# Transposing token tiles on VectorE in 32 by 32 blocks instead of on TensorE, in a cross-attention and expert-routing kernel

## The chip, the cores and the metric

The kernel runs on one core of a Trainium2 chip. The metric is the device time of one execution in microseconds. Engines are called by their names or as the profile shortens them: PE is TensorE (PEld its weight loads), DVE is VectorE, ACT is ScalarE, POOL is GpSimd, SP is SyncE, which issues most DMAs.

## The reference

Two blocks follow each other over x, four batches of 1024 tokens with 1024 features, all in float32. First an attention whose map comes from a context alone:

```python
query = einsum('bnc,dc->bnd', ctx, Wq) + bq          # 128 features
key = einsum('bnc,dc->bnd', ctx, Wk) + bk
attention = softmax(einsum('bnd,bmd->bnm', query, key))
x = x + einsum('bln,bmn->blm', layernorm(x), attention)
```

So a token's normed features are the contracted side, and each output feature m has a row of the attention. Then a mixture of experts on the normed x:

```python
xt = layernorm(x).reshape(4096, 1024)
scores = sigmoid(xt @ gate_w.T)                        # 8 experts
_, sel = top_k(scores + expert_bias, 2)
shared = (silu(xt @ sw1.T) * (xt @ sw3.T)) @ sw2.T     # hidden 704
routed = each chosen expert's swiglu of (score * xt), in bf16
x = x + shared + the routed rows added at their tokens
```

## The kernel before, in words

The tokens are 32 tiles of 128, worked in pairs g, g+1. The kernel has three stages: the attention (to about 621 us), the shared experts (eight blocks s of 512 tokens) and the routed experts (23 slots).

**Orders.** In the attention, the order of TensorE, GpSimd, VectorE and ScalarE is the order of the program text (manual_schedule, lines 218 and 553): each runs its instructions in order, and one that waits holds all that stand behind it. SP's DMAs there are ordered by the framework; in the shared experts SP's are in text order too.

**A pair.** product (line 399) multiplies a pair's two tiles, seen as a 2 by 2 block matrix, by the attention map, with seven block products instead of eight. seven (line 197) issues the seven steps k = 0 to 6, eight matmuls each, into three PSUM banks pa, pb, pc of which pa serves four times. After each step VectorE adds the bank's contents, times the token's inverse deviation rs, into the tile (line 410), and then between(k) puts other work in the text. A bank has one buffer, so the next use of it waits for that add. The step's stationary sides are the transposed tokens and sums of them: row_sums (line 391) makes three sums and a difference on GpSimd, of which step 1 needs the first. The products with the batch map need five such combinations of it: first_sums and second_sum on VectorE (lines 353, 360), last_sums on GpSimd.

**What rides along.** While batch b is multiplied, the map of batch b+1 is made: two 128-row strips a pair. For a strip, energies (line 317) puts four matmuls on TensorE and a row maximum nm on VectorE, softmax (line 326) is an exp with a sum on ScalarE, scaled (line 333) a reciprocal rc on VectorE and a product on ScalarE, turned (line 342) eight TensorE transposes in two PSUM tiles pt and two ScalarE copies out. Strip i is begun at the head of the pair, strip i+1 at k = 2; they are turned at k = 3 and 4. At a batch's first pair, queries makes the queries and keys first. In the last batch none of this is there.

**A tile's own path.** load brings x in. tokens (line 379) turns it on TensorE by transposed (line 250): for each half of the features four transposes into a PSUM tile pt (two buffers) and a ScalarE copy out. statistics (line 262) takes mean and variance on VectorE, and pow and a product on GpSimd give rs and nb; first_norm adds nb on ScalarE. After the product, stored (line 421) writes the tile to x2d in DRAM and takes its statistics; second_norm (line 426) makes the normed tile xt on ScalarE; turn (line 434) transposes xt on TensorE by the same helper into xtT, which is stored to xtd for the shared experts. gate_parts and gate (lines 444, 456) make the gate's logits from xtT with an eviction gs on ScalarE between them, route (line 460) the two chosen experts on VectorE, counts and lists_of their places in the lists. weighted (line 521) makes the two rows of each token, xt times its score, one on ScalarE and one on VectorE; scatter writes them to the lists with indirect DMAs.

**Conversions.** convert(e) (line 242) issues three DMAs on GpSimd's queue that read one expert's weights from DRAM in float32 and write them in bf16. Six experts are converted in the attention (pairs p = 1, 3, 5, 7, 10, 13, at k = 1), the other two in the shared experts at blocks s = 0 and 1 (line 1115).

**Lists read back.** From block 1 on, turns (line 978) gathers list rows with GpSimd's indirect DMAs (xgt), two ahead; VectorE reads the token number out of each (toks, line 999), and SP issues a transposing DMA. Two gathers are issued at the end of block 1's first half; the next ones in text order stand behind block 1's convert. Steps of turns stand between those of up (line 914).

Of the kernel before, what the change touches and what calls it, by code (L numbers as in the profile page):

```python
# [39 lines left out]
P = 128  # L41
# [21 lines left out]


# [13 lines left out]
def xattn_moe_kernel(ctx: ExitStack, tc: tile.TileContext, x, ctxT, wqT, wkT, bqk, gwT, ebias,  # L78
# [8 lines left out]
    x2d = dram.tile([T, D], F32, name="x2d")  # L87
# [137 lines left out]
    HALF, KH, M = KC // 2, NF // 2, NF * P  # L225
    LT = S // P
    with ExitStack() as a:
# [34 lines left out]
        def statistics(src, n):  # L262
# [9 lines left out]
            rs = sm.tile([P, 1], F32, tag="rs", name=f"rs_{n}", bufs=8)  # L272
            nc.gpsimd.tensor_tensor(rs, ve[:, 1:], const("half"), ALU.pow)  # L273
            nb = sm.tile([P, 1], F32, tag="nb", name=f"nb_{n}", bufs=8)
            nc.gpsimd.tensor_tensor(nb, ve[:, :1], rs, ALU.mult)
            return rs, nb
# [20 lines left out]
        def half_queries(b):  # L297
            for h in range(2):
# [13 lines left out]
                for i, to in enumerate((qs, ks)):  # L312
                    nc.vector.tensor_scalar_add(
                        to[b][:, cols], pq[:, i].rearrange("p j n -> p (j n)"), bqk_sb[:, i : i + 1])
# [57 lines left out]
        xin, xTs, x1s, xts, norms = {}, {}, {}, {}, {}  # L372

        def load(g):
            x1 = p3.tile([P, D], F32, tag="x1", name=f"x1_{g}", bufs=4)
            nc.sync.dma_start(x1, x[g * P : (g + 1) * P, :])
            xin[g] = x1

        def tokens(g):
            xTs[g] = [p3.tile([P, HALF, P], F32, tag=f"x{g % 2}{h}", name=f"xT_{g}_{h}")  # L380
                      for h in range(2)]
            transposed(xTs[g], xin[g], f"x{g}")

        def first_norm(g):

            x1 = xin.pop(g)
            rs, nb = norms.pop(g)
            nc.scalar.activation(x1, x1, AF.Identity, bias=nb)
            x1s[g] = x1, rs
# [31 lines left out]
        def stored(g):  # L421
            x1 = x1s[g][0]
            nc.sync.dma_start(x2d[g * P : (g + 1) * P, :], x1)
            norms[g] = statistics(x1, f"2_{g}")

        def second_norm(g):
            x2 = x1s.pop(g)[0]
            rs, nb = norms.pop(g)
            xts[g] = xt = p2.tile([P, D], F32, tag="xt", name=f"xt_{g}", bufs=4)
            nc.scalar.activation(xt, x2, AF.Identity, bias=nb, scale=rs)  # L430

        xtTs = {}

        def turn(g):

            if g % 2 == 0:
                xtTs[g] = p2.tile([P, KC, 2 * P], F32, tag="xtT", name=f"xtT_{g}", bufs=1)
            cols = slice(g % 2 * P, (g % 2 + 1) * P)
            xtT = xtTs[g - g % 2]
            transposed([xtT[:, :HALF, cols], xtT[:, HALF:, cols]], xts[g], f"t{g}")  # L440
            if g % 2:
# [79 lines left out]
        def weighted(g, i, ss):  # L521
            xt = xts.pop(g + i)
            rr = p2.tile([P, 2, ROW], BF16, tag="rr", name=f"rr_{g}_{i}")
            nc.scalar.mul(rr[:, 0, :D], xt, ss[:, 0, i : i + 1])
            nc.vector.tensor_scalar_mul(rr[:, 1, :D], xt, ss[:, 1, i : i + 1])
# [5 lines left out]
        def scatter(g, tois, rrs):  # L531
            for i in range(G):
                for k in range(2):
# [3 lines left out]
                        in_=rrs[i][:, k, :].bitcast(I32), in_offset=None)  # L537

# [13 lines left out]
        load(0)  # L552
        with tc.manual_schedule(engines=vector_scalar):
            ps_e = psum("ps_e", 3)
            for dst, k in ((trib, "tri"), (onesb, "ones")):
                nc.vector.tensor_copy(dst, const(k))
            halves = queries(0)
            tokens(0)
# [4 lines left out]
            nc.sync.dma_start(gw_sb[:, :, :E], gwT)  # L563

            sel = wp.tile([P, E], F32, name="sel")
            nc.vector.tensor_reduce(sel, ident.rearrange("p (j r) -> p r j", j=4)[:, :E, :], AX.X,
                                    ALU.add)
            eb_sb = wp.tile([P, E], F32, name="eb_sb")
            nc.sync.dma_start(eb_sb, ebias)
            next(halves)  # L570
            load(1)
            norms[1] = statistics(xin[1], "1_1")
# [11 lines left out]
            next(halves)  # L584
            first_sums(0)
# [4 lines left out]
            routing, listing, pair = {}, {}, {}  # L590
            for p in range(NT // 2):
# [19 lines left out]
                tokens(g + 1)  # L611
                first_norm(g + 1)
                a_units = row_sums(g)
# [6 lines left out]
                if p:  # L620
                    if ahead:
                        turn(g - 2)
                    second_norm(g - 1)
                if not new:
                    softened(i)

                def between(k):
                    if k == 0:
                        if not ahead:
                            turn(g - 2)  # L630
                        if new:
                            next(halves)
                        if p > 1:
                            pc_, ss, ohs = listing[g - 4]
                            listing[g - 4] = lists_of(g - 4, pc_, ohs), ss
                        if g + 2 < NT:
                            load(g + 2)
                            load(g + 3)
                        if g == NT - LT:
                            nc.sync.dma_start(sw13_sb, sw13)  # L640
                    elif k == 1:
# [3 lines left out]
                        if p:  # L645
                            turn(g - 1)
                        if ahead:
                            scaled(b + 1, i, on_scalar=True)
                        if p > 1:
                            tois, ss = listing.pop(g - 4)  # L650
                            listing[g - 4] = tois, [weighted(g - 4, j, ss) for j in range(G)]
                        if p in (1, 3, 5, 7, 10, 13):
                            convert((1, 3, 5, 7, 10, 13).index(p))
                    elif k == 2:
                        if not ahead:
                            pair[g] = gate_parts(g - 2)
                        looked(i + 1)
                        softened(i + 1)
                        if g + 2 < NT:
# [5 lines left out]
                    elif k == 3:  # L665
                        if p:
                            gs = gate_parts(g - 2) if ahead else pair.pop(g)
# [611 lines left out]
```

## Time and profile before

| | us |
|---|---|
| median of three runs | 1972.87 |
| lowest and highest | 1968.97, 1973.47 |
| the profiled execution, its time | 1973.84 |
| its span, first to last instruction | 1972.0 |
| TensorE busy in the span | 1940.1 |
| VectorE busy | 810.4 |
| ScalarE busy | 512.9 |
| GpSimd busy | 653.0 |

A group line of the profile gives source line, engine, operation, output tile and input tiles with their shapes, the count, then busy time in us, mean ns of one, and the idle time of the engine just before them with what ended it. A line of the order of time gives start and duration in us, engine, line and operation. A line of waits gives who waited for whom, us in total, how often, and the longest. A line of the table of stretches gives each engine's busy time and number of instructions in the stretch, TensorE's granted clock, the DMA engines' busy share and GB/s. Where a helper issues the work (line 129 for matmuls, line 256 for transposes, line 260 for their copies), tile names tell what it is: pt_x are transposes of x, pt_t of xt, pt_a of the attention.

### The profile page before, as it was taken

How to read it: one execution, taken by the hardware profiler on the slowest of the kernel's cores; microseconds unless marked ns; L12 is line 12 of the kernel's file. 1: busy time of each engine (PE TensorE's matmuls, PEld its weight loads, DVE VectorE, ACT ScalarE, POOL GpSimd, SP SyncE). 2: the span in 40 equal slices, each digit the busy share in tenths (PEclk: the TensorE clock that was granted, in tenths of full speed). 3: DMA queues.
4: the chain of work that ended last, by engine and by line, in shares of the span. 5: the costliest groups of instructions: out<-in, count | busy, mean ns of one | idle time of the engine just before them, and what ended most of it. 6: DMA issues, size and time to landing. Idle time of an engine off the chain costs nothing.

```text
span 1972.0 us, 23197 instructions
## 1 busy us (share of the span) xinstructions
PE 1940.1 (98%) x8480; PEld 1155.5 (59%) x8595; DVE 810.4 (41%) x1981; ACT 512.9 (26%) x884; POOL 653.0 (33%) x598
## 2 busy tenths in 40 slices
PE   8999999999999999999999999999999999999997
PEld 5655655655444447676676758584845555446564
DVE  5556566565875325423132323222233333223343
ACT  3344354355334101010111101010102233223242
POOL 0423533543642140313231222313014454425454
PEclk9999999999999999999999999999999999999999
DMA  3276485437685225397777868596464598649995
GB/s 124 65 194 169 167 220 158 154 129 206 246 228 203 98 75 141 94 238 205 202 187 191 206 179 224 153 173 193 121 265 107 114 311 275 140 131 326 342 357 98
DMA packets 225040, 365.48 MB, mean 185 GB/s; under 512 B 114080, under 2 KB 169888, under 8 KB 214048
## 3 DMA queue, kind: packets, MB, share of 16 engines
q0 software_dynamic: 43024, 172.78, 32.8%
q1 hardware_dynamic: 181904, 191.21, 32.0%
q8 instruction: 69, 1.13, 0.2%
q14 instruction: 43, 0.35, 0.1%
HBM read 289.19 MB, written 174.59 MB: 235 GB/s over the span
## 4 chain that ended last, share of the span: by engine, by line
PE 89%; DMA 5%; SPq 2%; DVE 2%; issue 1%; ACT 0%; POOL 0%; POOLq 0%; DVEq 0%; ACTq 0%
PE pa L129 19%; PE bank L129 15%; PE pc L129 10%; PE bank L1151 8%; PE qa L129 6%; PE pb L129 5%; DMA xh<-xgt 4%; PE pu L129 4%; PE pq L308 3%; PE pe L320 3%; PE qc L129 3%; PE pt_c L129 2%; PE pt_a L256 2%; SPq L1004 2%; PE qb L129 1%; PE pt_t L256 1%
## 5 line engine op out<-in xcount | busy, mean ns | idle before, releaser
L129 PE MATMUL bank<-xTb,w 128*128 128x0 bf16 x2024 | 311.6, 315 | 2.1 <-ACT sg_b L145 1.3
L129 PEld LDWEIGHTS <-w 128*128 128x128 bf16 x2024 | 190.5, 98 | 111.5 <-DVE hTb L1135 1.3
L749 POOL DMA_INDIRECT xgt<-xrows,li x92 | 88.8, 965 | 444.2 <-DMA xh<-xgt 211.6
L1184 POOL DMA_INDIRECT out_dram<-yt,toks x92 | 147.7, 1605 | 139.5 <-DVE yt L1180 80.8
L1151 PE MATMUL bank<-w,hTb 128*128 128x0 bf16 x920 | 164.5, 326 | 0.1
L273 POOL TENSOR_TENSOR rs<-ve,con 128x1 f32<-128x1 f32 x64 | 47.8, 747 | 313.7 <-DVE ve L271 313.7
L146 DVE TENSOR_TENSOR hTb<-sg_b,bank 128x512 bf16<-128x512 f32 x115 | 78.8, 688 | 161.5 <-PE bank L129 157.2
L129 PE MATMUL pa<-xs,sw_sb 128*128 128x256 f32 x560 | 132.3, 379 | 0.0
L1151 PEld LDWEIGHTS <-hTb 128*128 128x128 bf16 x920 | 72.4, 98 | 87.4 <-issue 11.7
L129 PE MATMUL pa<-aT,xT 128*128 128x512 f32 x256 | 116.8, 599 | 2.2 <-DVE x L410 2.0
L129 PEld LDWEIGHTS pa<-xs,sw_sb 128*128 128x128 f32 x560 | 106.4, 190 | 14.5
L145 ACT ACTIVATE sg_b<-bank 128x512 f32<-128x512 f32 x115 | 68.5, 597 | 165.8 <-PE bank L129 150.2
L1180 DVE COPY yt<-bank 128x512 f32<-128x512 f32 x92 | 61.3, 689 | 121.9 <-PE bank L1151 112.5
L1182 ACT COPY yt<-bank 128x512 f32<-128x512 f32 x92 | 53.3, 587 | 144.1 <-PE bank L1151 131.7
L749 POOL DMA_INDIRECT w<-w13b,wi x23 | 23.0, 999 | 201.4 <-PE bank L129 153.6
L534 POOL DMA_INDIRECT xrows<-rr,toi x64 | 64.9, 1015 | 60.9 <-issue 45.3
L410 DVE SCALAR_TENSOR_TENSOR x<-pa,rs,x 128x512 f32<-128x512 f32 x64 | 47.9, 748 | 88.8 <-PE pa L129 82.9
L166 ACT ACTIVATE st_c<-pt_c 64x256 f32<-64x256 f32 x7 | 2.6, 378 | 311.0 <-PE pt_c L129 311.0
L266 DVE BATCH_NORM_STATS2 st<-x 128x6 f32<-128x512 f32 x128 | 81.8, 681 | 0.6
L1032 DVE TENSOR_TENSOR x2c<-x2c,qa 128x512 f32<-128x512 f32 x64 | 43.8, 685 | 92.4 <-PE qa L129 92.4
L129 PE MATMUL pu<-xb,sw_sb 128*128 128x512 f32 x176 | 76.3, 593 | 0.9 <-PE pt_t L256 0.9
L941 DVE TENSOR_TENSOR one<-one,pb 128x256 f32<-128x256 f32 x35 | 14.7, 421 | 149.4 <-PE pb L129 140.1
(262 smaller groups left out, 3346.5 us busy)
## 6 DMA issues: line engine op xcount, KB each, us to landing
xturned<-xh SPq DMA_DIRECT2D x46, 512.0 KB
xTb<-xturned SPq DMA_DIRECT2D x23, 1024.0 KB
w13b<-in_w_dram POOLq DMA_DIRECT2D x8, 2816.0 KB
x<-in_x_dram SPq DMA_DIRECT2D x32, 512.0 KB
x2d<-x SPq DMA_DIRECT2D x32, 512.0 KB
xtd<-xtT SPq DMA_DIRECT2D x16, 1024.0 KB
xb<-xtd SPq DMA_DIRECT2D x8, 2048.0 KB
x2c<-x2d SPq DMA_DIRECT2D x16, 1024.0 KB
```

The costliest lines, as they stand in the source:

```text
L129: nc.tensor.matmul(part(pp), w(c), part(xT(c)), start=start and c == 0, stop=c == blocks - 1, skip_group_check=not start)
L145: nc.scalar.activation(sg, pa, AF.Silu)
L146: nc.vector.tensor_tensor(hT[:, f, :], sg, pb, ALU.mult)
L256: nc.tensor.transpose(pt[:, j, :], src[:, c * P : (c + 1) * P], ident)
L266: nc.vector.bn_stats(st[:, h, :], src[:, h * 512 : (h + 1) * 512])
L308: nc.tensor.matmul(pq[:, i, j, :], w[c // CH][:, c % CH, :], ct[c // CH][:, c % CH, :], start=c == 0, stop=c == CC - 1)
L320: nc.tensor.matmul(pe[:, h, :], qs[b][:, m * P : (m + 1) * P], ks[b][:, h * 512 : (h + 1) * 512], start=True, stop=True)
L534: nc.gpsimd.indirect_dma_start(out=places[2 * (g + i) + k], out_offset=bass.IndirectOffsetOnAxis(ap=tois[k][:, i : i + 1], axis=0), in_=rr ...
L749: nc.gpsimd.indirect_dma_start(out=dst, out_offset=None, in_=src, in_offset=bass.IndirectOffsetOnAxis(ap=idx, axis=0), **bound)
L1151: nc.tensor.matmul(part(py), hT[:, f, toks], part(w[:, f, cols]), start=False, stop=f == NF - 1, skip_group_check=q < 2)
L1180: nc.vector.tensor_copy(yt[:, q, h * 512 : (h + 1) * 512], py)
L1184: adds.append([nc.gpsimd.indirect_dma_start(out=outs[q], out_offset=bass.IndirectOffsetOnAxis(ap=toks[:, q : q + 1], axis=0), in_=yt[:, q, ...
```

## The change

The features' order in the transposed tiles is permuted so that a VectorE transpose, which turns each 32 by 32 block within its own 32 partitions, is enough. A tile is brought in a second time, quartered: partition 32j + a holds, for i = 0 to 3, the features of quarter j of token 32i + a. Turned block by block, partition 32j + f then holds feature 256j + 32c + f of all 128 tokens for c = 0 to 7. The weights that meet such features (gate, sw13) are loaded in that order, and the keys are written in it. For the second norm the quartered tile is read back from x2d, and normed by factors that a small matmul (spread) lays out for its partitions.

```diff
+CONVERT = (2, 6, 10, 13)
...
         def load(g):
-            x1 = p3.tile([P, D], F32, tag="x1", name=f"x1_{g}", bufs=4)
+            x1 = p2.tile([P, D], F32, tag="x1", name=f"x1_{g}", bufs=6)
...
+        def load_quarters(g):
+            xqs[g] = xq = p4.tile([P, 4, D // 4], F32, tag="xq", name=f"xq_{g}", bufs=2)
+            quarters_of(xq, x[g * P : (g + 1) * P, :])
+
+        def quarters_of(dst, src):
+
+            src = src.rearrange("(i a) (j f) -> j a i f", a=SQ, j=4)
+            for j in range(4):
+                nc.sync.dma_start(dst[j * SQ : (j + 1) * SQ], src[j])
+
         def tokens(g):
...
-            transposed(xTs[g], xin[g], f"x{g}")
+            src = xqs.pop(g).rearrange("p i (h c f) -> p h i c f", h=2, f=SQ)
+            for h, dst in enumerate(xTs[g]):
+                nc.vector.transpose(dst.rearrange("p c (i a) -> p i c a", a=SQ), src[:, h])
...
-        def second_norm(g):
-            x2 = x1s.pop(g)[0]
-            rs, nb = norms.pop(g)
-            xts[g] = xt = p2.tile([P, D], F32, tag="xt", name=f"xt_{g}", bufs=4)
-            nc.scalar.activation(xt, x2, AF.Identity, bias=nb, scale=rs)
...
+        def back(g):
+            ys[g] = y = p2.tile([P, 4, D // 4], F32, tag="y", name=f"y_{g}")
+            quarters_of(y, x2d[g // 2][g % 2 * P : (g % 2 + 1) * P, :])
+
+        def spread(g):
+
+            m = sm.tile([P, 2, 2, 4], F32, tag="m", name=f"m_{g}", bufs=2)
+            for v in range(2):
+                nc.vector.tensor_tensor(m[:, v], _bc(quarter, 1, [P, 2, 4]),
+                                        _bc(norms[g + v], 2, [P, 2, 4]), ALU.mult)
+            pt = ps_t.tile([P, 16], F32, tag="pt", name=f"sp_{g}")
+            nc.tensor.matmul(pt, fold, m.rearrange("p v r i -> p (v r i)"), start=True, stop=True)
+            spreads[g] = sp = sm.tile([P, 2, 2, 4], F32, tag="sp", name=f"sp_{g}", bufs=2)
+            nc.vector.tensor_copy(sp.rearrange("p v r i -> p (v r i)"), pt)
 
         def turn(g):
...
-            transposed([xtT[:, :HALF, cols], xtT[:, HALF:, cols]], xts[g], f"t{g}")
-            if g % 2:
+            xtT, sp, y = xtTs[g - v], spreads[g - v], ys.pop(g)
+            for i in range(4):
+                nc.scalar.activation(y[:, i], y[:, i], AF.Identity, bias=sp[:, v, 1, i : i + 1],
+                                     scale=sp[:, v, 0, i : i + 1])
+            nc.vector.transpose(
+                xtT[:, :, v * P : (v + 1) * P].rearrange("p c (i a) -> p i c a", a=SQ),
+                y.rearrange("p i (c f) -> p i c f", f=SQ))
+            if v:
                 nc.sync.dma_start(xtd[g // 2], xtT)
...
         def weighted(g, i, ss):
-            xt = xts.pop(g + i)
+            x2, rn = x1s.pop(g + i)[0], norms.pop(g + i)
+            w = sm.tile([P, 2, 2], F32, tag="w", name=f"w_{g}_{i}", bufs=4)
+            nc.vector.tensor_tensor(w, _bc(rn, 2, [P, 2, 2]), _bc(ss[:, :, i], 1, [P, 2, 2]),
+                                    ALU.mult)
             rr = p2.tile([P, 2, ROW], BF16, tag="rr", name=f"rr_{g}_{i}")
-            nc.scalar.mul(rr[:, 0, :D], xt, ss[:, 0, i : i + 1])
-            nc.vector.tensor_scalar_mul(rr[:, 1, :D], xt, ss[:, 1, i : i + 1])
+            for k in range(2):
+                nc.scalar.activation(rr[:, k, :D], x2, AF.Identity, bias=w[:, 1, k : k + 1],
+                                     scale=w[:, 0, k : k + 1])
...
+        def features(dst, src):
+
+            for j, h in itertools.product(range(4), range(2)):
+                nc.sync.dma_start(
+                    dst(slice(j * SQ, (j + 1) * SQ), slice(h * HALF, (h + 1) * HALF)),
+                    src[:, 2 * j + h, :].rearrange("(c f) n -> f c n", f=SQ))
...
             next(halves)
+            tokens(0)
+            tokens(1)
+            units = [row_sums(0)]
             first_sums(0)
             second_sum(0)
...
-                tokens(g + 1)
                 first_norm(g + 1)
-                a_units = row_sums(g)
...
-                if p:
-                    if ahead:
-                        turn(g - 2)
-                    second_norm(g - 1)
...
                         if g + 2 < NT:
-                            load(g + 2)
-                            load(g + 3)
+                            for h in (g + 2, g + 3):
+                                load(h)
+                                load_quarters(h)
                         if g == NT - LT:
-                            nc.sync.dma_start(sw13_sb, sw13)
+                            features(lambda j, c: sw13_sb[j, c], sw13)
                     elif k == 1:
...
                         if p:
-                            turn(g - 1)
+                            spread(g - 2)
                         if ahead:
                             scaled(b + 1, i, on_scalar=True)
...
-                        if p in (1, 3, 5, 7, 10, 13):
-                            convert((1, 3, 5, 7, 10, 13).index(p))
+                        if p in CONVERT:
+                            convert(CONVERT.index(p))
                     elif k == 2:
-                        if not ahead:
-                            pair[g] = gate_parts(g - 2)
                         looked(i + 1)
                         softened(i + 1)
+                        if p:
+                            turn(g - 2)
                         if g + 2 < NT:
                             norms[g + 2] = statistics(xin[g + 2], f"1_{g + 2}")
...
                     elif k == 3:
-                        if p:
-                            gs = gate_parts(g - 2) if ahead else pair.pop(g)
...
                         if ahead:
                             turned(b + 1, i)
                             scaled(b + 1, i + 1, on_scalar=True)
                         if p:
-                            gate(lg, gs)
-                            routing[g - 2] = route(g - 2, lg)
+                            turn(g - 1)
                         if p > 1:
-                            scatter(g - 4, *listing.pop(g - 4))
+                            scatter(g - 4, listing.pop(g - 4), rows.pop(g - 4))
                         if g + 2 < NT:
                             norms[g + 3] = statistics(xin[g + 3], f"1_{g + 3}")
                     elif k == 4:
                         if ahead:
                             turned(b + 1, i + 1)
+                        if p:
+                            lg = ps_s.tile([P, G, E], F32, tag="lg", name=f"lg_{g}")
+                            gate(lg, gate_parts(g - 2))
+                            routing[g - 2] = route(g - 2, lg)
                     elif k == 5:
                         if g + 2 < NT:
                             tokens(g + 2)
+                            first_norm(g + 2)
+                        if p:
+                            rows[g - 2] = [weighted(g - 2, 0, routing[g - 2][1])]
...
+                    elif k == 6:
+                        back(g)
+                        back(g + 1)
+                        if g + 2 < NT:
+                            tokens(g + 3)
+                            units[0] = row_sums(g + 2)
                         if p:
                             mask, ss, ohs = routing.pop(g - 2)
                             pc_ = ps_s.tile([P, 2, G, E], F32, tag="lg", name=f"pc_{g}")
                             counts(pc_, mask)
...
+                            rows[g - 2].append(weighted(g - 2, 1, ss))
...
+            next(ups)
+            spread(g)
+            next(ups)
             turn(g)
...
             turn(g + 1)
-            scatter(g - 2, tois, [weighted(g - 2, j, ss) for j in range(G)])
+            nc.vector.tensor_tensor(ws[0], w21, w22, ALU.add)
             next(ups)
             lg = bank("lg_last")[:, : G * E].rearrange("p (g e) -> p g e", g=G)
             gate(lg, gate_parts(g))
-            nc.vector.tensor_tensor(ws[0], w21, w22, ALU.add)
...
             if s < 2:
-                convert(E - 2 + s)
+                convert(E - 4 + 2 * s)
+                convert(E - 3 + 2 * s)
```

## The prediction

> **What bounds the kernel now.** I read the page first, then the stretch table over single pairs of token tiles, TensorE's waits, the groups by form, and the order of time in one pair. Of the stretch table, a pair with the next batch's attention riding along, and a pair of the last batch:
>
> ```profile
> core 0: us, PE busy (x) PEld busy (x) DVE busy (x) ACT busy (x) POOL busy (x), PEclk, DMA share, GB/s
> ...
> 402.00:437.00 35.00, 35.00 (x140) 18.43 (x139) 21.44 (x64) 18.09 (x28) 12.37 (x17) 1.00 0.34 123
> ...
> 563.00:592.00 29.00, 29.00 (x107) 14.34 (x106) 19.36 (x60) 11.09 (x16) 11.96 (x16) 1.00 0.80 246
> ```
>
> TensorE is busy throughout at full clock (so it is through the shared experts, 529.55 of 530 us), VectorE 61 to 67% of a pair. TensorE's waits from 0 to 625 us, all of them:
>
> ```profile
> PE pq L308 <- DMA ct<-in_ctxT_dram: 4.7, 2, 4.2
> PE pt_a L256 <- DVE at L340: 2.4, 2, 1.8
> PE pa L129 <- DVE x L410: 2.0, 1, 2.0
> PE pc L129 <- POOL s L176: 1.4, 1, 1.4
> ```
>
> (and two of 1.4 and 0.4). So TensorE alone sets the pace, and what leaves it pays only while VectorE and ScalarE, which are in order, keep up. Groups by form (busy us, mean ns of one after the bar):
>
> ```profile
> L266 DVE BATCH_NORM_STATS2 st<-x 128x6 f32<-128x512 f32 x128 | 81.8, 681 | 0.6
> ...
> L323 DVE TENSOR_REDUCE nm<-pe 128x1 f32<-128x1024 f32 x32 | 39.2, 1224 | 14.0 <-PE pe L320 13.6
> ...
> L256 PE MATMUL pt_t<-con,xt 128*128 128x128 f32 x256 | 33.2, 273 | 1.2 <-ACT xt L430 1.2
> L256 PE MATMUL pt_x<-con,x 128*128 128x128 f32 x256 | 33.2, 273 | 0.0
> ```
>
> **What TensorE loses.** The 512 transposes pt_x and pt_t stand in 64 runs of eight. A run shows 1.04 us, but the next step's matmuls start 0.88 us after it begins (95.62 pe to 97.34 pt_t to 98.21 pa in the order of time), as the ends overlap. 64 x 0.88 = 56 us, 3.5 us a pair. Added: one 16-column matmul a pair (about 0.2 us).
>
> **What VectorE gets.** A pair gains four transposes of 512 elements a partition and two of 1024, two products m, a copy sp and two products w; it loses two rr of 0.75 us. No row shows a VectorE transpose. Near rows: f32 passes at one element a step, 0.68 us for 512 (two run in 1.28) and 1.22 for 1024. The Trainium skill, "VectorE: DVE Perf Modes", The three transpose paths, speaks against the change: for 128x128 bf16 it gives 390 ns on TensorE and 311 on VectorE and says to use TensorE for that shape where PSUM will do. The trace differs on the first: 0.11 us, eight in 0.88. By the page's two prices the change would take 512 x 0.39 = 200 us off TensorE and put 512 x 0.311 = 159 on VectorE; by the rows it is 56 off and 16 x (4 x 0.6 + 2 x 1.2) = 77 on. I take the rows (0.6 and 1.2) because the passes are long, and keep twice that, near the page's 311 ns per 128 elements, as upper bound. The lower one is the fastest f32 pass there is, at by rc (L340), 0.75 us for 1024 and half of it for 512.
> ScalarE loses eight evictions and two xt, gains eight 256-wide passes y and two rr: about neutral, 18 us of 35. A 128x256 activation takes 0.417 us alone (L942's row); overlapped (two 0.588 us copies run in 1.07) four take 1.5 us, bounds 1.1 and 1.7.
>
> **Where it lies: walking one pair.** Order of time in the pair at 410 us: what the later walk needs on ScalarE and VectorE.
>
> ```profile
> 415.65 1.23 DVE L323 TENSOR_REDUCE nm<-pe 128x1 f32<-128x1024 f32 x1 [0.97 <-PE pe L320]
> ...
> 416.91 1.11 ACT L329 ACTIVATE at<-pe,nm 128x1024 f32<-128x1024 f32 x1 [2.66 <-DVE nm L323]
> ...
> 421.72 1.15 ACT L338 ACTIVATE at<-at,rc 128x1024 f32<-128x1024 f32 x1
> ```
>
> Between them the statistics follow nm at once (416.79), and rc stands at 419.75. The scaled at is ready at 422.9 and TensorE transposes it from 424.5: 1.6 us to spare. Now with the new order, t = 0 when step 2's matmuls start; a step is 3.43 us, the energies 1.72.
> - TensorE: step 2 to 3.43, energies to 5.15, step 3 to 8.58, turned(i) to 9.45, step 4 to 12.9.
> - VectorE: nm done 6.5; exp with its accumulator done 7.8 on ScalarE; only behind it turn(g-2)'s four passes, to 9.3; VectorE waits for them, transposes to 10.5, statistics (1.85) to 12.4, step 3's add 13.1, rc 13.25; at scaled 14.45. turned(i+1) stalls **1.6 us**, runs to 15.6.
> - turn(g-1): four passes to 15.95, transpose to 17.2. gate_parts stalls **1.6 us**, to 18.3. gate follows its own eviction gs (0.37) with nothing between, as turned lay before: **0.6 us**. Step 5 from 19.3, step 6 ends 26.2.
> - VectorE from 17.2: statistics 19.05, add 19.75, route (3.7) 23.45, add 24.15, statistics 26.0, tokens 27.2, w and cast 27.6, step 6's add 28.3, statistics 30.15, tokens 31.35, w 31.7, nm 32.85.
> - TensorE: energies to 27.9; step 0 needs the bank that the 28.3 add frees (**0.4**); step 1 needs GpSimd's first row sum, 1.3 us after 31.35 (**1.1**), and ends at 36.3.
> - spread: its matmul needs m, which stands on VectorE behind step 1's add: 0.2 + 0.7 + 0.4, **1.4 us** in every pair; everything of step 2 is queued behind it. Step 2 starts at 37.9.
>
> A pair takes 37.9 us instead of 34.6: 6.7 of new waits and spread's 0.2 against 3.5 saved, **+3.3**. Ten intervals between step 2 of neighbouring pairs up to the last batch: +33 us (those with queries too: their extra matmuls cover the two small waits, but spread also waits for an nm there). The first interval, with no turn, gains 1.4; the beginning 1 (two runs gone, the row sums later); the end 2 (two runs into the shared weights).
> Into the last batch first_sums and second_sum (2.28 us each) stand between those adds on VectorE, with no queries to cover them: the bank at 30.5, the row sum at 36.5 beside second_sum, step 2 near 41.8 against 34.8, **+7**. In the last batch no exp stands before the passes: the walk gives 30.9 against 29.55 (step 0's bank 2, row sum 1, gs 0.6, spread 1.4, less 3.5): +1.3 twice, and nothing for its first, where a 4.37 us rr beside GpSimd's sums goes away and the casts beside them stay. Attention: -1 - 1.4 + 33 + 7 + 3 - 2 = **+39**.
>
> **The converts.** Two experts' conversions leave the attention, where the queue cost TensorE nothing, and go to the shared experts, where two are issued together. GpSimd's order of time around the second place now:
>
> ```profile
> 827.44 0.75 POOL L243 DMA_DIRECT2D w13b<-in_w_dram  x1
> ...
> 829.59 1.03 POOL L749 DMA_INDIRECT xgt<-xrows,li  x1 [0.30 <-issue]
> 830.92 1.00 POOL L749 DMA_INDIRECT xgt<-xrows,li  x1 [0.30 <-issue]
> 859.57 0.95 POOL L749 DMA_INDIRECT xgt<-xrows,li  x1 [27.65 <-DMA xh<-xgt]
> ```
>
> The gathers of 829.6 and 830.9 queue behind the conversion on the one software queue; its packets run from 830 to 857 (27 us), and the third toks, at 862.1, just finds its rows. With two they land at 884 or later: VectorE stands at 862.1 for 22 us. TensorE goes on through steps 5 and 6 and two steps of the next block, to 868.4, then needs ScalarE, which waits for VectorE: **+18 us** (bounds 0, if the gathers pass, and 25, if stores slow the second conversion). The first place has no gather behind it: DMA idles there from 768 to 800.
>
> **Other edits at nothing.** The second load of x and the read back of x2d (33 MB, 1 KB pieces): the first has 20 us to its use, the second 12 or more; without that cover a late y stalls turn. SP issues 16 more DMAs a pair, 0.33 us each, 5 us of 35, in front of xtd's store and the next loads, none urgent. The eight-piece sw13 load has 100 us. kT's scattered write keeps its 0.74 us. The earlier ws[0] sum lies in ups beside 13.7 us blocks. GpSimd's pow stays; the routed experts are untouched. A late landing of these costs up to 10 us in all; a gain there has no wait to come from.
>
> **Sum.** 1973.84 (this execution, span 1972.0) + 39 + 18 = 2030.8; it lies 1.0 over the median 1972.87, so **2030 us**.
>
> **Rivals.**
> 1. Attention slows, but the gathers don't stand behind the second conversion: 1973 + 39 = 2012. Against it: one software queue, and GpSimd's wait of 27.7 us in that place. 15%.
> 2. Transposes at twice the cost: 4.8 us a pair more on the same loop, 16 x 4.8 = 77, so 2107. For it the page's 311 ns. 8%.
> 3. Faster. TensorE stays the bound: passes, transposes and statistics hide under steps 3 and 4. It decides where the new waits fall below 3.5 us a pair less what the converts cost; with waits of 1.5 it gains 2 x 16 = 32, so 1959 with the 18 us of the converts, 1941 without. VectorE's busy sum, 21.4 - 1.5 + 5.7 = 25.6 of 31, would allow it; the in-order chain says no, since spread, scaled and gate wait by program order. 10%.
> 4. Both effects cancel, within 0.3%: 5%.
> The forecast's own case has the remaining 62%, 1995 to 2060 by the bounds of passes (-13), transposes (-27), converts (-18 to +7) and late data (+10), not all at once. 0.3% is about what a measurement of this kernel can tell from no change. The range, 1980 to 2095, reaches part of the way into 2 and leaves out the rest of it, 3 and most of 4. Faster 0.10, same 0.05, slower 0.85.
>
> **What would show it.** TensorE's waits from 0 to 650 us should name sp or m (about 1.4 us x 15), pt_a on at, gp on xtT and lg on gs, and pairs near 38 us apart. If pairs are 31 to 33 us apart, the walk is wrong. toks should show one wait of over 20 us near the shared experts' third block, with TensorE idle some 18 us. Transposes should read 0.6 to 0.68 and 1.15 to 1.25 us. It fails if ScalarE's four passes come in under 1 us, or transposes run at two elements a step.

## The result, and the profile after

The changed kernel takes **2185.6 us** (median of four runs, 2182.5 to 2188.2) against 1972.4 for the kernel before, a ratio of 1.108 [1.107, 1.110]. The direction was as predicted; the size, +213 us instead of +57, lies well outside the range of 1980 to 2095.

From the page of the changed kernel: span, TensorE's busy time, and the granted clock by fortieths of the span.

```profile
span 2181.9 us, 22813 instructions
...
PE 1964.6 (90%) x8000; PEld 1131.5 (52%) x8115; DVE 866.4 (40%) x2129; ACT 514.8 (24%) x884; POOL 645.9 (30%) x598
...
PEclk9999998898988899999899999999999999999999
```

TensorE has lost 512 transposes and yet is busier than before (1940.1): its clock is below full through the attention (mean over the whole span 0.953, before 0.996). TensorE's waits, in us in total, times and longest:

```profile
PE pa L135 <- DVE x L431: 43.8, 13, 14.8
PE sp L460 <- DVE m L457: 40.8, 16, 11.5
PE gp L485 <- DVE xtT L473: 22.5, 10, 2.2
PE pt_a L263 <- ACT at L346: 18.5, 11, 1.7
PE pq L314 <- DMA ct<-in_ctxT_dram: 14.6, 2, 10.5
PE pa L135 <- ACT one L986: 13.8, 2, 13.2
```

Where the prediction showed four small waits there are now six large ones: sp, gp and pt_a are the waits it named, and the first row, step 0's bank, is several times what it gave it (0.4 us in a regular pair). The middle of one pair, TensorE's order of time:

```profile
330.99 1.09 PE L263 MATMUL pt_a<-con,at 128*128 128x128 f32 x8 [1.68 <-ACT at L346]
334.33 1.94 PE L485 MATMUL gp<-xtT,gw_sb 128*32 128x256 f32 x16 [2.25 <-DVE xtT L473]
336.75 1.02 PE L493 MATMUL lg<-fold,gs 128*128 128x8 f32 x4 [0.48 <-ACT gs L488]
337.62 6.40 PE L135 MATMUL pc<-aT,s 128*128 128x512 f32 x8
...
351.13 3.70 PE L135 MATMUL pa<-aT,xT 128*128 128x512 f32 x8 [1.83 <-DVE x L431]
...
361.62 0.40 PE L460 MATMUL sp<-m,fold 128*128 128x16 f32 x2 [2.17 <-DVE m L457]
```

The reader should see two things. The waits stand where the walk put them. And step 5 (337.62), which waits for nothing, takes 6.40 us where a step took 3.6 in the kernel before. The table of stretches gives the reason, TensorE's granted clock, third from the end: it is halved here. The other two rows are step 2 at the head of this pair and of the next, 5.38 and 3.68 us long, each behind a wait of 2.17 us:

```profile
332.90:343.00 10.10, 8.19 (x27) 3.85 (x28) 6.78 (x25) 2.54 (x6) 2.68 (x4) 0.50 0.47 186
...
314.48:319.69 5.21, 5.21 (x10) 2.20 (x10) 0.24 (x2) 1.15 (x1) 0.00 (x0) 0.67 0.68 167
361.87:365.38 3.51, 3.51 (x10) 1.60 (x10) 0.24 (x2) 1.15 (x1) 0.00 (x0) 1.00 1.10 247
```

Step 2 of the first pair starts 11.9 us later than before; over the sixteen pairs 171 us more are lost (regular pairs, the eight away from the first pair, the changes of batch and the last batch, take 44.8 to 47.4 us, 45.7 on average, instead of 34.6), and some 27 behind the attention, 16 of them at the converts.

### The profile page after: what moved, and what is told of

It reads as the page before. It is cut to its first block, busy times and chain, and to the rows that moved or that the text cites. A ratio compares the mean times of both kernels' runs of the same rounds, so it can differ in the third digit from the quotient of the medians.

```text
span 2181.9 us, 22813 instructions
## 1 busy us (share of the span) xinstructions
PE 1964.6 (90%) x8000; PEld 1131.5 (52%) x8115; DVE 866.4 (40%) x2129; ACT 514.8 (24%) x884; POOL 645.9 (30%) x598
## 4 chain that ended last, share of the span: by engine, by line
PE 57%; DMA 4%; issue 1%; DVE 1%; SPq 1%; ACT 0%; POOL 0%; POOLq 0%; DVEq 0%; ACTq 0%
PE bank L135 13%; PE pa L135 10%; PE bank L1203 7%; PE qa L135 5%; PE pc L135 5%; PE pu L135 4%; PE pb L135 3%; PE qc L135 2%; DMA xh<-xgt 2%; PE pt_c L135 2%; PE qb L135 1%; DMA w<-w13b,wi 1%; PE qc L1079 1%; PE qb L1079 1%; PE qc L1073 1%
## 5 line engine op out<-in xcount | busy, mean ns | idle before, releaser
L280 POOL TENSOR_TENSOR rn<-ve,con 128x1 f32<-128x1 f32 x64 | 35.5, 555 | 493.8 <-DVE ve L278 493.8
L135 PE MATMUL pa<-aT,xT 128*128 128x512 f32 x256 | 123.7, 629 | 43.5 <-DVE x L431 43.5
L563 ACT ACTIVATE rr<-x,w 128x1024 bf16<-128x1024 f32 x64 | 75.9, 1233 | 207.6 <-DVE w L559 176.6
L1203 PEld LDWEIGHTS <-hTb 128*128 128x128 bf16 x920 | 72.1, 97 | 86.1 <-issue 10.1
L135 PEld LDWEIGHTS pa<-aT,xT 128*128 128x128 f32 x256 | 49.5, 201 | 104.0 <-issue 52.8
L135 PE MATMUL pc<-aT,s 128*128 128x512 f32 x128 | 85.7, 832 | 0.0
```

The costliest lines, as they stand in the source:

```text
L135: nc.tensor.matmul(part(pp), w(c), part(xT(c)), start=start and c == 0, stop=c == blocks - 1, skip_group_check=not start)
L563: nc.scalar.activation(rr[:, k, :D], x2, AF.Identity, bias=w[:, 1, k : k + 1], scale=w[:, 0, k : k + 1])
L1203: nc.tensor.matmul(part(py), hT[:, f, toks], part(w[:, f, cols]), start=False, stop=f == NF - 1, skip_group_check=q < 2)
```

## The experiments

Ratios are to the kernel before, with 95% intervals.

| kernel | us | ratio |
|---|---|---|
| e1 token number ahead of the passes | 2119.1 | 1.075 [1.073, 1.077] |
| e2 converts as before | 2164.2 | 1.097 [1.095, 1.099] |
| e3 spread's factors early | 2158.1 | 1.094 [1.092, 1.096] |
| e4 waits filled | 2191.5 | 1.110 [1.107, 1.112] |
| e5 waits filled by half | 2148.0 | 1.089 [1.087, 1.091] |
| e6 reordered | 2074.8 | 1.053 [1.051, 1.055] |
| e7 tokens' half alone | 1967.1 | 0.997 [0.996, 0.998] |
| e8 attention results' half alone | 2136.0 | 1.084 [1.082, 1.086] |
| e9 e6, converts at k = 1 | 2035.4 | 1.033 [1.031, 1.035] |
| e10 e9, transfers spread | 1974.9 | 1.002 [1.001, 1.003] |
| e11 e10, banks exchanged | 1973.6 | 1.000 [0.999, 1.001] |
| e12 e7, banks exchanged | 1966.8 | 0.997 [0.996, 0.998] |

**e1.** Why does step 0 wait for VectorE's add? The order of time where the add of step 6 is due, all engines:

```profile
347.68 0.12 DVE L559 TENSOR_TENSOR w<-rn,ss 128x4 f32<-128x4 f32 x1
347.84 2.37 ACT L563 ACTIVATE rr<-x,w 128x1024 bf16<-128x1024 f32 x2 [8.82 <-DVE w L559]
350.24 0.18 DVE L565 CAST rr<-con 128x32 int32<-128x32 f32 x1 [2.44 <-ACT rr L563]
```

The token number (L565) goes into the same tile rr as ScalarE's two rows and stands behind them, so VectorE, which is in order, waits 2.44 us twice a pair, with step 6's add behind it. The edit puts its write first:

```diff
+            nc.vector.tensor_copy(rr[:, :, D:].bitcast(I32), ...)
             for k in range(2):
                 nc.scalar.activation(rr[:, k, :D], x2, ...)
-            nc.vector.tensor_copy(rr[:, :, D:].bitcast(I32), ...)
```

> The changed kernel, with the small write of the token number into rr put ahead of ScalarE's two passes over rr instead of behind them. In the changed kernel's order of time this write stands 2.44 us on VectorE behind those passes, twice in each of 15 pairs, and everything after it on VectorE is late by as much. Theory A (in-order waits set the pace, and this is one of them, which the prediction left out): 15 x 4.9 = 73 us go, and up to 2 us a pair more of slow clock, so about 2185 - 73 to - 105 = 2080 to 2112. Theory B (VectorE's added work as such sets the pace): the wait fills with other VectorE work already late, and the time stays above 2160.

It gained 66 us: regular pairs went from 45.7 to 41.6 us on average, and step 0's waits from 43.8 to 17.6, with the longest of 14.8 falling to 5.4. spread's wait fell too, from 2.17 to 1.1 us in a regular pair. B falls. The gain is 7 us short of A's, and step 5 still took 5.1 to 6.6 us: the slow step is not this wait's doing.

**e2.** Conversions at the places of the kernel before.

```diff
-CONVERT = (2, 6, 10, 13)
+CONVERT = (1, 3, 5, 7, 10, 13)
...
-                convert(E - 4 + 2 * s)
-                convert(E - 3 + 2 * s)
+                convert(E - 2 + s)
```

> The changed kernel with the conversions where they were before (pairs 1, 3, 5, 7, 10, 13, and one each in shared blocks 0 and 1). Theory A (gathers queue behind the second conversion: toks waits 18.3 us, TensorE 13.2 and 2.9 of slow clock): 16 us go from the shared experts, about 2169, and toks' wait of 18 us is gone. Theory B (more conversions beside the attention's extra loads hold up y or rr there): the attention gets longer by 10 us or more, and the time stays at 2180 or above.

21 us gained, as A had it; the longest wait of toks went from 18.3 to 5.9 us, and TensorE's wait for ScalarE's `one` is gone.

**e3.** The products m, which spread's matmul needs, are made at k = 0 instead of just ahead of it.

```diff
-        def spread(g):
-
-            m = sm.tile([P, 2, 2, 4], F32, tag="m", name=f"m_{g}", bufs=2)
...
+        def factors(g):
+
+            ms[g] = m = sm.tile([P, 2, 2, 4], F32, tag="m", name=f"m_{g}", bufs=2)
...
+        def spread(g):
+
+            m = ms.pop(g)
...
+                        if p:
+                            factors(g - 2)
```

> The changed kernel with the products m for spread made at k = 0, behind step 0's add, instead of k = 1; spread's matmul stays. Theory A (each in-order wait counts by itself): spread's wait of 2.2 us in 15 pairs (11.5 in the first of the last batch, which partly stays) goes, with some slow clock: 2185 - 33 to - 55 = 2130 to 2152. Theory B (VectorE is the loop's bound, so that the wait moves to the next place where TensorE needs it): within 10 us of 2185.

27 us, 6 short of A's nearest figure; B falls. spread's wait fell from 2.17 to 0.33 us, and step 2, which had taken 5.38 us in every second pair, took 3.68 in all regular pairs: more than the wait's own 1.84 us came back where the clock had fallen too. Part of the gain went again to step 0's waits, which rose from 43.8 to 51.1 us.

**e4 and e5.** Is it the clock that makes steps slow? Unused matmuls of 256 columns are put ahead of the two waits at k = 4, 8 and 10 of them in e4, 4 and 5 in e5; the rest is as in the changed kernel.

```diff
                     elif k == 4:
+                        fill(8)      # e5: fill(4)
                         if ahead:
                             turned(b + 1, i + 1)
+                        fill(10)     # e5: fill(5)
```

> The changed kernel with 18 matmuls of 256 columns that compute nothing used, in the pairs that make the next batch's attention: 8 ahead of turned(i+1) at k = 4 and 10 behind it, 1.7 and 2.2 us, where TensorE waits 1.7 and 2.25 us. Theory A (the waits let TensorE's clock fall, and the matmuls after them run slow: step 5 takes 6.0 us instead of 3.4, step 2 of every other pair 5.4): with TensorE kept busy the steps are back at 3.4 us, 3 to 5 us a pair in 11 pairs, and the time falls by 25 to 50 us although work was added. Theory B (those steps are slow for what they read, not for the clock): the time stays or rises by up to 20 us, and step 5 still shows 6 us.

> The changed kernel with 4 and 5 unused matmuls of 256 columns in place of the 8 and 10 of the run before it, which took 0.43 us each, twice what was reckoned, so that they lasted 7.9 us where the waits are 4. Theory A (slow clock after waits): step 5 stays at 3.4 us and nothing is added beyond the waits, so 2.9 us in step 5 and 1 in gp and lg go in 11 pairs, less 1.7 where step 0 goes slow in its turn: 2185 - 24 to - 43 = 2142 to 2161. Theory B (the clock follows the mean load, so that what is gained here is lost in other steps): within 10 us of 2185.

I had mis-sized the fill: one took 0.43 us, twice what I reckoned, so e4 put in more work than there was waiting and came out 6 us slower in the median, with runs from 2183 to 2196. e5 gained 38 us with work added, as its A said. In e5's order of time, the step that had taken 6.40 us:

```profile
320.95 0.61 PE L493 MATMUL lg<-fold,gs 128*128 128x8 f32 x4 [0.48 <-ACT gs L488]
321.41 3.68 PE L135 MATMUL pc<-aT,s 128*128 128x512 f32 x8
```

Its row in the table of stretches shows the clock at full:

```profile
321.41:324.93 3.52, 3.52 (x10) 1.61 (x10) 2.93 (x16) 1.22 (x2) 0.28 (x2) 1.00 0.60 230
```

In e4 step 5 was equally fast, and step 0, behind its unfilled wait of 2.11 us, took 5.40 in several pairs. So the slowness follows the waits and not the instruction. But the length of a wait does not decide alone: behind the same 2.11 us step 0 took 5.40 in some pairs of e5 and 3.70 in others, as step 2 did behind 2.17 us in the changed kernel. What decides between them was not tested.

**e7 and e8.** Each half alone: e7 is the kernel before with the tokens' transposes on VectorE; e8 the changed kernel with these on TensorE again.

> The kernel before with the x half of the change alone: x loaded a second time in quarters, turned by VectorE, keys in that order; xt stays on TensorE, nothing else moves. Theory A (what costs is the y path: passes, spread, gate and rr, which this half has not): 32 runs of eight leave TensorE, 28 us, and 2.5 us of VectorE a pair lie in its free third: 1943 to 1955. Theory B (any transposes on VectorE hold up the bank's adds and the row sums): 1972 or more.

> The changed kernel with x turned by TensorE again: no second load of x, keys in natural order; all of the y path stays. TensorE gets 28 us back; VectorE loses 2.5 us a pair of the stretch that makes step 0, step 1 and spread wait (1.83, 0.92, 2.17 us). Theory A (most of the loss is the y path): 2140 to 2185. Theory B (the x half causes half of it): under 2100.

e7 brought the reckoned 1.75 us a regular pair (32.83 against 34.58) and 9 us by the first up product, but ended only 5 us ahead, short of A: the start waits for the context (10.9 us in all), and GpSimd's row sums and step 0's bank bind in the first pair and the last batch. e8 got faster although TensorE took 28 us of transposes back, 4 us beyond A's range and far from B's. So the attention results' way, with the waits it makes, carries most of the loss: 164 of the 213 us by itself. The halves do not add up, though: -5 and +164 leave some 55 us that come only when both are there, 14 of them before step 2 of the first pair (71.1 us in e8, 85.1 with both).

**e6.** All the late orders undone at once, nothing left out: m at k = 0; the four passes for both tiles at k = 1, the transposes behind them at k = 2; gate_parts at k = 3; statistics later; e1's order; both token tiles at k = 5; conversions of the attention as in the kernel before, but at k = 3 behind the scatters; and the gate weights' eight loads behind the first context loads.

> The whole change, with the order of its steps altered: token number ahead of rr's passes; m at k = 0; ScalarE's passes over y at k = 1, transposes at k = 2, gate_parts at k = 3 ahead of turned, gate behind turned at k = 4; both token tiles turned and the row sums made at k = 5; the second norms' statistics at k = 6, lists at k = 3; conversions at the old pairs but at k = 3 behind the scatters, one each in shared blocks 0 and 1; the gate's weights loaded behind the first contexts. Theory A (the loss is waits in program order and the clock that follows them, not VectorE's load of 25.6 us a pair): pairs take 31 to 33 us, TensorE's 56 us come back, and the time is 1915 to 1950, under the kernel before. Theory B (VectorE's load is too much for a pair of 31 us): pairs stay at 35 us or more and the time above 1985.

111 us gained, yet the time is above A's range and past B's bound of 1985 us. B's figure holds and its reason does not: undisturbed pairs took 32.6 us, less than the 34.6 of the kernel before, at full clock. Around a conversion gp waited 6.3, 13.2, 13.9 and 15.4 us, and at two changes of batch pq waited 18.5 and 19.3 us for the context. One of gp's waits in the order of time:

```profile
326.22 2.07 ACT L476 ACTIVATE y<-y,sp 128x256 f32<-128x256 f32 x4 [13.91 <-DMA y<-x2d]
328.32 1.25 DVE L485 STREAM_TRANSPOSE xtT<-y 128x1024 f32<-128x1024 f32 x1 [13.77 <-ACT y L476]
...
332.07 1.93 PE L497 MATMUL gp<-xtT,gw_sb 128*32 128x256 f32 x16 [13.16 <-DVE xtT L485]
```

Read from below: TensorE waits for the transpose, that for the passes, those for the read-back of x2d.

**e9.** e6 with the conversions at k = 1, behind lists made at k = 0 and scatters at k = 1.

> The whole change with the reordered steps, once more; the six conversions of the attention are issued at k=1 instead of k=3, behind the pair's scatters, which move up to k=1 with their lists at k=0 (last_sums follows the scatters). Nothing is left out. Theory A (in the reordered kernel the attention's results came back late only where a conversion's transfers lay over the reads of y and of the context): the 13 to 15 us waits of gp on xtT (50.1 us) and of pq on ct (43.6 us) go but for a few us, every pair takes 32.5 to 34.5 us, the first up product starts at 605 to 630 us instead of 719, and the time is 1950 to 1990 us. Rival B (the way by way of DRAM, or SyncE's order of issues, is too long by itself and the conversion only stood beside it): gp's waits on xtT stay at several us in most pairs or move to other pairs, and the time is above 2020 us.

40 us gained, above A's range and in B's: y was still late behind conversions. One pair with a conversion, in the kernel before and then, with the pair that follows, in e9 (the last two columns are the DMA engines' busy share and GB/s):

```profile
258.33:292.91 34.58, 34.58 (x135) 18.02 (x135) 21.03 (x65) 17.67 (x27) 11.97 (x16) 1.00 0.95 237
```

```profile
260.43:293.06 32.63, 31.56 (x107) 14.78 (x106) 23.90 (x73) 17.81 (x26) 13.69 (x19) 1.00 1.05 263
293.06:334.00 40.94, 33.61 (x108) 15.96 (x106) 23.89 (x73) 17.94 (x26) 11.92 (x16) 0.92 0.73 207
```

In this pair the conversion had the 16 DMA engines full already before the change (0.95). It takes 29 us to land in e9, and its tail, with the pair's new loads, ran into the read-back, which the next pair needs at its k = 1. Of gp's 46.0 us in e9, 31.9 stand in one place, at 605.85, where the conversion of p = 13 follows the shared expert's eight loads.

**e10.** A conversion's 2816 KB part and its 1408 KB rest in different pairs, and the shared expert's eight loads half in pair 12, half in 13.

```diff
+CONVERT = (1, 2, 4, 6, 8, 10), (3, 5, 7, 9, 11, 14)
...
-                        if g == NT - LT:
-                            features(lambda j, c: sw13_sb[j, c], sw13)
+                        if b + 1 == B and i < G * 2:
+                            features(lambda j, c: sw13_sb[j, c], sw13, (i, i + 1))
```

> The previous kernel (the whole change with reordered steps and conversions at k=1) with the transfers spread out: a conversion's large first part (2816 KB, 22 us to land) and its rest (1408 KB) are issued in different pairs, and the shared expert's eight loads go half into pair 12 and half into pair 13. No work is added, left out or moved between engines. Theory A (the attention's results are read back late because a pair with a whole conversion already keeps the 16 DMA engines 95% busy in the kernel before, and the second read of the tokens and the results' read-back have no room left beside it): gp's waits on xtT fall from 46 us to under 8, pq's waits on ct from 26 us to under 8, no pair shows a DMA share near 1, the first up product starts at 615 to 635 us instead of 695.6, and the time is 1945 to 1985 us. Rival B (SyncE's issues, eight reads at 0.5 us for each batch of results ahead of the context's loads, are what makes them late): the waits stay within a third of their size (gp at 30 us or more, ct at 17 or more) and the time is above 2010 us.

60 us gained, no work removed. The edit spreads two things at once, the conversions and the eight loads, and no run tells their shares apart. TensorE's waits in e10:

```profile
PE pa L135 <- DVE x L438: 23.4, 13, 6.2
PE pq L322 <- DMA ct<-in_ctxT_dram: 14.2, 5, 4.5
...
PE gp L504 <- DVE xtT L492: 1.4, 3, 0.6
```

gp's waits fell from 46.0 us to 1.4: SyncE issues as many reads as in e9, so B falls. y took 5.0 us at most to land between 150 and 560 us (8.5 in e9). Two of A's figures were missed: the context's waits stayed at 14.2, and single pairs still show a DMA share of 0.94 to 1.02, this one with no slow step in it:

```profile
292.90:325.50 32.60, 31.54 (x106) 14.77 (x105) 23.87 (x73) 17.77 (x27) 12.65 (x18) 1.00 1.02 264
```

A full pair is thus not harmful in itself; what is left as the cause is what stands in front of a transfer that is needed soon.

e10 is still no faster than the kernel before. Its eight regular pairs (32.6 to 33.3 us) gain 14 us on it; at the two changes of batch 8 us go again (52.4 and 52.2 us against 48.4; TensorE waits 4.2 and 4.5 us there for the context), and some 7 in the way into the last batch, in it and at its end.

**e11 and e12.** The largest wait left in e10 is step 0's for VectorE's last add. One line exchanges pa and pb in every second pair:

```diff
-            pa, pb, pc_ = (... for k in ("pa", "pb", "pc"))
+            pa, pb, pc_ = (... for k in (("pa", "pb", "pc") if g % 4 else ("pb", "pa", "pc")))
```

> The previous kernel (whole change, reordered, conversions split) with one line changed: in every second pair the names of the accumulators pa and pb are exchanged, so that step 0 of a pair sums in a bank that the last pair left after its step 3, not in the one that VectorE empties after step 6. Nothing is left out. Theory A (what remains in the way is step 0's wait for VectorE's last add: 1.07 us in a regular pair, 2.8 to 6.2 in the last batch with a slow step 0 of 5.4 us after it; 23.4 us of waits and some 8 us of slow steps): pa's waits on x vanish, regular pairs take 31.5 to 31.8 us, the first up product starts at 603 to 610 us instead of 636.4, and the time is 1938 to 1955 us, below the kernel before. Rival B (VectorE has that work to do in any case and the wait comes up at the next thing TensorE needs of it: the spread, the turned columns, step 1): a gain under 10 us, time above 1965 us.

> The kernel before with the tokens' half alone (as in the tokens-only kernel), and the same exchange of pa and pb in every second pair. Nothing is left out. Theory A (the tokens-only kernel lost its gain in part to step 0's waits of 8.5 us in the last batch and a slow step after them): 1953 to 1962 us; the waits of pa on x vanish. Rival B (VectorE's lateness moves to the next need): 1964 to 1970 us, as without the exchange. Against the kernel of theory A's other run it tells whether the way of the attention's results by DRAM, once it is no longer in the way, is worth anything by itself: if the whole change is at least 8 us faster than this one, it is.

Theory A falls in both: pa's waits went, but not the time. In e11 the first up product starts at 626.8 us and in e10 at 626.7 (the expectation's 636.4 is the second one, behind spread). The row of pa is gone, and its place is taken:

```profile
PE pq L322 <- DMA ct<-in_ctxT_dram: 16.3, 5, 4.6
PE sp L474 <- DVE m L467: 11.7, 12, 3.6
PE gp L504 <- DVE xtT L492: 8.3, 8, 2.2
```

In e12 the 8.5 us of pa are gone, and the wait for GpSimd's row sum grew from 2.0 to 10.9 us. The bank was only where VectorE's lateness was met first. The whole change in its best order (e11) equals the kernel before; the tokens' half alone (e7, e12) is 0.3% faster, the only version that beats the kernel before. The attention results' half gained nothing on top of it: e11 is 6.8 us slower than e12.

## Why the prediction was wrong, step by step

In short: of the walk through a pair, what failed is VectorE's "w and cast 27.6" (66 us by e1) and "A step is 3.43 us" carried through new waits (38 us or more by e5). Other parts of the 156 us missed are single places that were put at nothing, and two sizes. These shares overlap, and no run adds them up.

**Right.** What binds: TensorE's time is worth nothing while in-order engines keep it waiting. The named waits came where they were put: turned(i+1) 1.68 us (1.6 predicted), gate_parts 2.25 (1.6), gs 0.48 (0.6), the row sum 0.92 (1.1), spread 2.17 (1.4). The converts: toks waited 18.3 us (22) and TensorE 13.2 with 2.9 of slow steps after it, 16 in all (18):

```profile
1069.98 0.16 DVE L1050 TENSOR_TENSOR toks<-xgt,beyond 128x1 int32<-128x1 int32 x1 [18.28 <-DMA xgt<-xrows,li]
...
1071.24 3.78 PE L135 MATMUL pa<-xs,ws 128*128 128x256 f32 x8 [13.16 <-ACT one L986]
```

The durations of the transposes, where the rows were taken against the page's price, from the groups of the changed kernel:

```profile
L403 DVE STREAM_TRANSPOSE xT<-xq 128x512 f32<-128x512 f32 x64 | 41.6, 689 | 0.8 <-issue 0.4
L473 DVE STREAM_TRANSPOSE xtT<-y 128x1024 f32<-128x1024 f32 x32 | 39.6, 1241 | 71.3 <-ACT y L471 71.3
```

0.69 and 1.24 us, against 0.6 and 1.2 taken; 81 us on VectorE in all, 77 reckoned. With these durations rival 2 falls, and with toks' wait rival 1.

**Wrong, 1: "VectorE from 17.2 ... w and cast 27.6" in the walk.** The cast of the token number was counted with its own duration and not with what it waits for: rr's two ScalarE passes. 4.9 us a pair on VectorE, step 0's bank at 1.83 us instead of "0.4", and with it spread's 2.17 us, which fell to 1.1 in e1. e1 measured this step at 66 us, peaks in the last batch included. The rule that I stated for m and gs (who stands behind the wait) I didn't apply to the row that had changed engines.

**Wrong, 2: the sum had no term for the clock.** "A step is 3.43 us" was carried through the walk, though the walk itself put new waits of 1.6, 1.6 and 0.6 us within 8 us. In the pair shown, step 5 took 2.8 us more than its usual 3.6, gp and lg 1.4, and step 2 takes 1.7 more in about every second pair: 3.2 us of the 10.2 that a pair of 44.8 us lost, and 5.9 of the 12.8 in one of 47.4. e5 shows 38 us of it as the least, since its fill cost time too. The Trainium skill, "TensorE: Matmul & The Clock Gate", HAM oscillation, warns of single idle gaps of over about 3.4 us, which halve the clock; no regular pair has one, the longest is 2.31. By the rule nothing would have been added. By the runs shorter waits can be enough: the clock was at half from 332.9 us on, behind the wait of 1.68 us and within that of 2.25.

**Wrong, 3: "other edits at nothing", "up to 10 us in all".** The gate weights' eight loads were not named there. SyncE stood 8.6 us, to 17.1, for VectorE, which clears their tile at 16.84, and issued them ahead of the next context loads (21.34 us instead of 10.53), so that TensorE waited 10.48 us. It is the order of issues that costs and not the loads: e8 has the same eight, its context loads went ahead at 9.40, and this wait isn't there. At p = 13 the scatters of rr queued behind a conversion, so that ScalarE's next rr waited 17.22 us, VectorE's cast 13.21 and TensorE 14.77: the mechanism that I had used for the gathers, not looked for at the scatters. At p = 12 two casts of 4.2 us beside GpSimd's sums, "the casts beside them stay", held m, and TensorE waited 11.55 us.

**Wrong, 4: sizes.** Four passes took 2.06 us, not 1.5 and above the bound of 1.7; that accounts for most of the 0.65 us by which gate_parts' wait was too small.

Together, a regular pair: 3.3 predicted, 1.4 for the bank, 0.8 for spread, 0.65 for gate_parts and 3.2 or 5.9 for the clock make 9.4 and 12.1 of the 10.2 and 12.8 measured; the rest was not placed. The rivals: the faster one rested on the passes and transposes hiding under TensorE's steps. In e6, reordered so that they do (at k = 1 and 2), undisturbed pairs take 32.6 us, so its mechanism exists, but not in the order of the change.

What stays open: when a wait of about 2 us costs clock and when it doesn't; some 10 us behind the attention, besides the converts, of which 3.7 are spread's last wait; and the waits for the context that e11 still has.

## What to carry to other kernels

When work moves to an in-order engine, list for every instruction that shares a tile with it which engine finished that tile last; a small write behind another engine's long one costs its whole duration, and all that stands behind it. Before a sum is trusted at full clock, add up the new waits within a step or two and look at the granted clock behind waits of that length, and before a transfer through DRAM is called hidden, look at what is in the queues when it is issued, not at the average share. Removing the wait that comes first only pays if the engine behind it is early enough for the next one: exchanging two banks took 23 us of waits away and moved the time by 1 us, within the noise.

## What the runs showed of the hardware that was not expected

Behind a wait of 1.68 us and within the next, of 2.25, the granted clock fell to 0.50 and stayed there for 10.1 us, so that the next step took 6.4 us instead of 3.7; unused matmuls in these waits kept it at 1.00 and made the kernel 38 us faster. A wait of 2.17 us cost clock in some pairs (0.67 over the next step) and none in others (1.00). VectorE casts of two elements a partition took 4.2 us while a GpSimd tensor_tensor of 4.5 us ran (0.17 in e10, where none did). Conversions, scatters and gathers, all issued by GpSimd, came in each other's way: 18.3 us for a gather, 17.2 us for the buffer of a scatter.
